# The joint pass of a four-layer graph network: sources turned on VectorE, joins and range sums as bf16 thirds, first MLP products in one bf16 pass

## The chip, the cores and the metric

The kernel runs on one core of one Trainium2 chip. The time is the device time of one execution in microseconds (us), the median of the runs of that kernel. A profile is one further execution with the hardware profiler on; its length is given beside the others, since here it differs from them. Engines: TensorE (matmul, with its weight loads apart), VectorE, ScalarE, GpSimd (which here only issues indirect DMAs), and SP, the queue that issues the plain DMAs.

## The reference

12,500 nodes with 32 features, 400,000 edges sorted by their target `dst`. Four layers, each on a normalised copy `h` of `x`, each added to `x`:

```python
h = jnp.maximum(_layernorm(x, axis=-1), 0.0)
x = x + _L0_gnn_ref(h, edge_attr_32, L0_gnn_eps, src, dst)
h = jnp.maximum(_layernorm(x, axis=-1), 0.0)
x = x + _L1_gnn_ref(h, src, dst, edge_attr_3, edge_attr_10, edge_weight, L1_gnn_W1, L1_gnn_W2)
h = jnp.maximum(_layernorm(x, axis=-1), 0.0)
x = x + _L2_gnn_ref(h, src, dst)
h = jnp.maximum(_layernorm(x, axis=-1), 0.0)
x = x + _L3_gnn_ref(h, src, dst, edge_attr_4, edge_attr_8, L3_gnn_fc_w1, L3_gnn_fc_w2)
```

Layer 1 (an equivariant convolution) is the heavy one. For every edge a small MLP makes 896 weights, which are contracted with the features of both ends and the edge's direction:

```python
h = 2.0 ** 0.5 * jax.nn.relu(emb @ W1 / 10.0 ** 0.5)
w = (h @ W2 / 16.0 ** 0.5).reshape(E, 7, MUL, MOUT)
...
edge_ftr = jnp.concatenate([s_act, (gates[:, :, None] * v_out).reshape(E, 24)], axis=1) * norm[:, None]
return jax.ops.segment_sum(edge_ftr, edge_dst, num_segments=N)
```

Layer 2 is a normalised sum in the other direction: each edge adds the scaled features of its target to its source, `segment_sum(xs[edge_col], edge_row)` with `edge_row = src` and `edge_col = dst`.

## The kernel before

Edges are padded to 196 chunks of 2048. A chunk is 16 groups of 128 edges, or four sets (`Q4`) of `B` = 512. Since edges are sorted by target, the targets of a chunk lie within 128 successive node rows, its *window*: sums by target are matmuls with a one-hot matrix `oh` into that window, and target features come from the window by a matmul with the one-hot matrix `has`. Sources are anywhere: they are gathered by indirect DMA, 128 rows each (`hs`), and layer 2's sums by source are scattered by indirect DMA with accumulation into four tables. [...] the group is first *joined*: a 128 x 128 matrix `eq` says which edges share a source, a matmul with it gives each the sum, and all but the first are sent to a spare row.

The program has three stretches: layer 0 (with `rest`, a generator of preparations that is advanced beside its loop), the joint pass of layers 1 and 2 (`edges12`), and layer 3. The change lies in the joint pass and in `rest`.

`edges12` is unrolled over the chunks and software-pipelined by hand. A round is twelve steps `s`. In round c, chunk c (`now`) gets its twelve `product(c, j, h)`: two matmuls of 64 input rows into `ps_y`, and the multiplication by `hid` into `z` on VectorE; `reduce` sums `z` over the MLP's units with four matmuls into `ps_o`. Chunk c-1 (`last`) gets `back`: `rows`, `gate`, `collect` (the sum into the window), `add`. Chunk c+1 (`next_`) gets `front`: `has`, `ends`, `times_n`, `hidden`. `gather` issues the 16 gathers of chunk c+3. Layer 2 follows behind: chunk c-3 (`close`) gets `near` (the normalisation of its window) and `lay` (target features to edges, `hd`), chunk c-4 (`far`) gets `second`: `alike` makes `eq` and the row numbers, `join` does the matmuls and evicts `summed`, `scatter` issues the 16 scatters one round later. The order on each engine is not quite that of the text: the framework that builds the program orders the instructions of each engine by a model of its own, so that GpSimd, for one, issues 16 gathers and then 16 scatters.

The parts that the change touches:

- `ends` (L718 and on): the 16 gathered groups are turned to features x edges by fp32 matmuls with the unit matrix `eye` (L723), into rows 0-31 and 64-95 of `ps_m`; target features come into rows 32-63 and 96-127 by matmuls with `has` (L727); ScalarE copies the whole to `X[:, h]` (L729). The product `Q` = `N` x `X` follows (L732).
- `hidden` (L739, L741): the MLP's first layer from `emb`, four sets of 10 rows in fp32 at partitions 0, 32, 64 and 96.
- `alike` (L871) with `firsts` (L449 to L456): `eq`, the count `cnt` of earlier equal edges through `tmp`, and the rows.
- `join` (L879, L881): fp32 matmuls of `eq` (128 x 128) with `hd` (32 columns), evicted by ScalarE.
- `collect` (L789): fp32 matmuls of `f` (32 columns as weights) with `oh` (128 columns), four column groups summed apart; `add` (L795 to L799) folds the four.

Tiles of PSUM: `ps_y` has two buffers of two banks; `ps_m`, `ps_o`, `ps_sum` and `ps_2` one bank each.

## Time and profile before

| | us |
|---|---|
| median of 3 runs | 19167.42 (19167.29 to 19172.29) |
| the profiled execution | 23109.4 |
| its span, first to last instruction | 23107.7 |

Over the span of the profiled execution TensorE is busy 15954.9 us (69%), its weight loads 8493.8, GpSimd 14407.0 (62%), VectorE 11868.8 (51%), ScalarE 5515.5 (24%); the mean granted TensorE clock is 0.828 of full speed. Busy time adds up instructions; it does not say which of them the end waited for. The chain of waits that ended last puts 39% on TensorE, 18% on VectorE, 9% on ScalarE and 5% on GpSimd. The profiled execution is a fifth longer than the runs, so a sum made in it has to be carried over with care.

An fp32 matmul appears as two records in the trace, a bf16 one as one; so 3136 x 2 records of L879 are 3136 matmuls.

### The profile page before, as it was taken

What the parts mean: (1) busy time and instruction counts of PE and PEld (TensorE: products, weight loads), DVE (VectorE), ACT (ScalarE), POOL (GpSimd) and SP (SyncE); (2) the same over time, 40 slices, a digit from 0 to 9 for tenths busy, and PEclk for the clock granted to TensorE, in tenths of its full rate; (3) what the DMA queues carried; (4) which work ended last, traced back from release to release, by engine and by line L of the source; (5) the groups of instructions that cost most, each with busy time, mean ns of one, the idle gap of its engine ahead of it and who ended that gap; (6) DMA issues with size and microseconds to landing.
All of it is one profiled execution on the core that took longest, in us unless ns stands there. A gap on an engine that the chain in (4) does not pass through costs nothing.

```text
span 23107.7 us, 229565 instructions
## 1 busy us (share of the span) xinstructions
PE 15954.9 (69%) x74484; PEld 8493.8 (37%) x74484; DVE 11868.8 (51%) x24410; ACT 5515.5 (24%) x12954; POOL 14407.0 (62%) x12552
## 2 busy tenths in 40 slices
PE   2333333328888778778777777787588888888887
PEld 2333333322333333333333333333355445445544
DVE  4443333335555555555555555555455555555555
ACT  0000000002222222222222222222233333333333
POOL 5666666655777777777777777777444444444443
PEclk9999999998777777777777777777687888888887
DMA  2111111113333333333333333333100000000000
GB/s 74 42 35 23 23 23 23 23 40 73 80 80 79 77 78 83 77 78 82 80 78 81 80 77 79 78 83 77 24 12 12 12 12 12 12 12 12 12 12 18
DMA packets 1503407, 1138.52 MB, mean 49 GB/s; under 512 B 1141492, under 2 KB 1304900, under 8 KB 1448308
## 3 DMA queue, kind: packets, MB, share of 16 engines
q1 hardware_dynamic: 745098, 891.46, 12.3%
q0 software_dynamic: 752640, 206.32, 9.7%
q10 hardware_dynamic: 4448, 25.89, 0.3%
q8 instruction: 592, 9.70, 0.2%
q14 instruction: 629, 5.15, 0.1%
HBM read 1022.56 MB, written 99.86 MB: 49 GB/s over the span
## 4 chain that ended last, share of the span: by engine, by line
PE 39%; DVE 18%; another core or an unknown queue 15%; issue 11%; ACT 9%; POOL 5%; DMA 2%; DVEq 0%; SPq 0%; POOLq 0%; ACTq 0%
PE ps_y L746 11%; PE ps_w L1162 10%; PE ps_o L756 4%; PE ps L879 4%; ACT oh L781 3%; DVE z L749 3%; DVE rb L1180 3%; POOL hs L433 2%; DVE pb L1172 2%; PE ps_h L1140 2%; ACT oh L710 2%; PE ps_win L385 2%; PE ps_sum L1201 1%; DVE f L1178 1%
## 5 line engine op out<-in xcount | busy, mean ns | idle before, releaser
L885 POOL DMA_INDIRECT acc<-summed,rows x3136 | 4995.6, 1593 | 1898.0 <-issue 1141.3
L1130 POOL DMA_INDIRECT hs<-feat,src x3136 | 3085.0, 984 | 3653.4 <-DVE pb L1172 2657.8
L1162 PE MATMUL ps_w<-w2b,hid 128*128 128x256 f32 x12544 | 4006.1, 462 | 608.6 <-issue 430.0
L433 POOL DMA_INDIRECT hs<-feat,src x3136 | 3136.5, 1000 | 1881.0 <-issue 864.2
L704 POOL DMA_INDIRECT hs<-feat,src_c x3136 | 3189.0, 1017 | 1126.7 <-issue 932.0
L1162 PEld LDWEIGHTS ps_w<-w2b,hid 128*128 128x128 f32 x12544 | 2722.3, 227 | 2283.9 <-issue 1572.6
L749 DVE TENSOR_TENSOR z<-ps_y,hid 128x1024 f32<-128x1024 f32 x2352 | 2842.0, 1218 | 1235.5 <-PE ps_y L746 1007.3
L385 PE MATMUL ps_win<-m,oh 128*128 128x32 f32 x6272 | 1488.0, 402 | 2521.3 <-ACT m L561 1829.8
L746 PE MATMUL ps_y<-X,w2t 64*128 64x512 f32 x4704 | 2258.9, 838 | 613.4 <-ACT hid L741 306.4
L385 PEld LDWEIGHTS ps_win<-m,oh 128*128 128x128 f32 x6272 | 1398.1, 328 | 2612.4 <-ACT m L561 1921.6
L1167 DVE TENSOR_TENSOR pa<-ps_w,q 128x512 f32<-128x512 f32 x784 | 536.0, 684 | 3153.4 <-PE ps_w L1162 2928.4
L756 PE MATMUL ps_o<-z,sums 128*32 128x512 f32 x9408 | 1936.9, 697 | 2.5 <-issue 1.6
L746 PE MATMUL ps_y<-Q,w2t 64*128 64x512 f32 x4704 | 1688.5, 740 | 83.6 <-DVE z L749 39.8
L723 PE MATMUL ps_m<-eye,hs 128*32 128x128 f32 x6272 | 805.2, 367 | 1048.3 <-ACT X L729 790.5
L879 PEld LDWEIGHTS ps<-hd,eq 128*128 128x128 f32 x6272 | 1048.0, 253 | 1241.9 <-issue 339.4
L879 PE MATMUL ps<-hd,eq 128*128 128x32 f32 x6272 | 1144.2, 335 | 513.7 <-DVE eq L871 197.1
L732 DVE TENSOR_TENSOR Q<-N,X 128x512 f32<-128x512 f32 x392 | 271.6, 693 | 2115.6 <-ACT X L729 1473.0
L1142 ACT ACTIVATE hid<-ps_h 128x1024 f32<-128x1024 f32 x784 | 799.8, 1020 | 2236.2 <-PE ps_h L1140 1651.5
L1172 DVE TENSOR_TENSOR pb<-ps_w,hs 128x256 f32<-128x256 f32 x3136 | 1281.8, 469 | 0.0
L1140 PE MATMUL ps_h<-emb,w1q 8*128 8x512 f32 x3136 | 1066.5, 761 | 230.0 <-DMA emb<-in_ea_c 165.1
L746 PEld LDWEIGHTS ps_y<-X,w2t 64*128 64x128 f32 x4704 | 603.4, 236 | 1658.0 <-issue 742.6
L723 PEld LDWEIGHTS ps_m<-eye,hs 128*32 128x32 f32 x6272 | 546.2, 147 | 1635.2 <-ACT X L729 929.7
(191 smaller groups left out, 18563.7 us busy)
## 6 DMA issues: line engine op xcount, KB each, us to landing
has<-loc_t SPq DMA_DIRECT2D x392, 1024.0 KB
srow<-in_src_t SPq DMA_DIRECT2D x392, 512.0 KB
hs<-feat,src POOLq DMA_INDIRECT x6272
N<-n_t SPq DMA_DIRECT2D x3136, 32.0 KB
edge_attr<-in_edge_attr SPq DMA_DIRECT2D x196, 256.0 KB
hs<-feat,src_c POOLq DMA_INDIRECT x3136
acc<-summed,rows POOLq DMA_INDIRECT x3136
emb<-in_ea_c SPq DMA_DIRECT2D x784, 20.0 KB
```

What stands on the lines that cost most here:

```text
L385: nc.tensor.matmul(c["sum"], lhsT=oh[:, k, :], rhs=feat[:, k, :], start=t0 + k == 0, stop=t0 + k == self.CT - 1)
L433: self.nc.gpsimd.indirect_dma_start(out=t[:, k, :], out_offset=None, in_=self.feats[l][:], in_offset=bass.IndirectOffsetOnAxis(ap=idx[:, t ...
L704: nc.gpsimd.indirect_dma_start(out=c["hs"][:, k, :], out_offset=None, in_=self.feats[1][:], in_offset=bass.IndirectOffsetOnAxis(ap=c["src_ ...
L746: nc.tensor.matmul(y[:, q, :], lhsT=self.w2t[64 * q : 64 * q + 64, j, :], rhs=c["Q" if j < 3 else "X"][64 * q : 64 * q + 64, h, :], start= ...
L749: nc.vector.tensor_mul(z, y, c["hid"][:, 2 * h : 2 * h + 2, :])
L756: nc.tensor.matmul(c["o", j // 3][32 * q : 32 * q + 32, :], lhsT=self.sums[:, j, :], rhs=c["z", j, q // 2][:, q % 2, :], start=j % 3 == 0, ...
L879: nc.tensor.matmul(t[:, k, :], lhsT=c["eq"][:, k, :], rhs=c["hd"][:, G * g + k, :], start=True, stop=True)
L885: nc.gpsimd.indirect_dma_start(out=self.tabs[2][k % NTAB][:], out_offset=bass.IndirectOffsetOnAxis(ap=c["rows"][:, G * g + k : G * g + k + ...
L1130: nc.gpsimd.indirect_dma_start(out=c["hs"][:, k, :], out_offset=None, in_=self.feats[3][:], in_offset=bass.IndirectOffsetOnAxis(ap=c["src" ...
L1140: nc.tensor.matmul(t[:, q, :], lhsT=self.w1q[r : r + 8, m * P : (m + 1) * P], rhs=c["emb"][r : r + 8], start=True, stop=True)
L1162: nc.tensor.matmul(w[:, k, :], lhsT=c["hid"][:, m, 4 * g + k].rearrange("p q s -> p (q s)"), rhs=self.w2b[:, m, :], start=m == 0, stop=m == 1)
L1172: nc.vector.tensor_mul(c["pb"][:, i, gs], w[:, :, lo : lo + 64].rearrange("p g (w u) -> p g w u", u=8), by[:, :, None, :].to_broadcast([P, ...
```

## The change

**Sources.** The turning by `eye` goes. VectorE transposes the gathered tile in 32 x 32 blocks, the whole of it into each half of `X`; the target rows are then written over by ScalarE. Half of the 32-row blocks belong to each side, and which edges lie where now alternates: in `X[:, 1]` the source rows are those that hold targets in `X[:, 0]`. So `w2t` gets a second copy with the sides exchanged, and the sets of a half are q = h, h + 2. Gathers use the layout of `src`, which `alike` needs too, so one load serves both.

**Thirds.** An fp32 number is split into three bf16 numbers that sum to it: a copy, a subtraction, a copy, a subtraction (`thirds` for `f`, `split` for `hd`). `eq` and `oh` are exact in bf16. A join is then one bf16 matmul with 96 columns, and a reduction over the three parts on VectorE evicts it; a range sum is one bf16 matmul with 96 weight columns, and `fold` sums the three parts.

**First MLP products.** `parts_of`, a part of `rest` in layer 0, writes the thirds of `emb` to DRAM nine times (3 parts x 3), `stacked` does the like with the weights, and `hidden` multiplies 90 bf16 rows at once.

```diff
+    def parts_of(self, pool, src, dst):
+        ...
+        for k in range(0, flat.shape[1], F):
+            ks = slice(k, k + F)
+            v = pool.tile([P, 2240], F32, name="pv", bufs=2)[:, :F]
+            nc.sync.dma_start(v, flat[:, ks])
+            yield
+            p = [pool.tile([P, 2240], BF16, name=f"pp{i}")[:, :F] for i in range(3)]
+            nc.scalar.copy(p[0], v)
+            nc.vector.tensor_tensor(v, v, p[0], op=ALU.subtract)
+            yield
+            nc.scalar.copy(p[1], v)
+            nc.vector.tensor_tensor(p[2], v, p[1], op=ALU.subtract)
+            for i in range(3):
+                for j in range(3):
+                    nc.sync.dma_start(outs[3 * i + j][:, ks], p[i])
+            yield
...
-                c["emb"] = ld.tile([P, B], F32, name="emb")
-                for q in range(Q4):
-                    nc.sync.dma_start(c["emb"][32 * q : 32 * q + 10],
-                                      self.a["ea10_c"][q, :, ds(row, 1), :].rearrange("f o e -> f (o e)"))
+                c["emb"] = ld.tile([90, Q4 * B], BF16, name="emb")
+                nc.sync.dma_start(c["emb"], self.emb10[:, :, ds(row, 1), :].rearrange("k f o e -> (k f) (o e)"))
...
-            def ends(c, h):
+            def sources(c, h):
+                nc.vector.transpose(c["X"][:, h, :], c["hs"].rearrange("p t f -> p (t f)"))
+
+            def targets(c):
                 t = ps.tile([P, B], F32, name="ps_m")
-                for k in range(4):
-                    for q in range(2):
-                        nc.tensor.matmul(t[64 * q : 64 * q + 32, k * P : (k + 1) * P],
-                                         lhsT=c["hs"][:, 4 * (2 * h + q) + k, :], rhs=self.eye, start=True, stop=True)
-                for q in range(2):
-                    e0 = (2 * h + q) * B
-                    nc.tensor.matmul(t[64 * q + 32 : 64 * q + 64, :], lhsT=c["win"], rhs=c["has"][:, e0 : e0 + B],
+                for g in range(Q4):
+                    b = g ^ 1
+                    nc.tensor.matmul(t[32 * g : 32 * g + 32, :], lhsT=c["win"], rhs=c["has"][:, b * B : (b + 1) * B],
                                      start=True, stop=True)
-                nc.scalar.copy(c["X"][:, h, :], t)
+                for g in (1, 3, 0, 2):
+                    nc.scalar.copy(c["X"][32 * g : 32 * g + 32, (g ^ 1) % 2, :], t[32 * g : 32 * g + 32, :])
...
-                    r = 32 * (2 * h + q)
-                    nc.tensor.matmul(t[:, q, :], lhsT=self.w1t[r : r + 10], rhs=c["emb"][r : r + 10],
-                                     start=True, stop=True)
+                    e0 = (2 * q + h) * B
+                    nc.tensor.matmul(t[:, q, :], lhsT=self.w1t, rhs=c["emb"][:, e0 : e0 + B], start=True, stop=True)
...
-                    j = 32 * (k % 4)
-                    nc.tensor.matmul(c["sum"][j : j + 32, 0:P], lhsT=c["f"][:, k, :], rhs=c["oh"][:, k, :],
-                                     start=k < 4, stop=k >= CT - 4)
+                    nc.tensor.matmul(c["sum"][: 3 * D, 0:P], lhsT=c["f3"][:, k].rearrange("p i f -> p (i f)"), rhs=c["oh"][:, k, :],
+                                     start=k == 0, stop=k == CT - 1)
...
+            def split(c, step):
+
+                if step == 0:
+                    c["hd3"] = sp.tile([P, CT, 3, D], BF16, name="hd3")
+                if step % 2 == 0:
+                    nc.scalar.copy(c["hd3"][:, :, step // 2, :], c["hd"])
+                elif step == 1:
+                    nc.vector.tensor_tensor(c["hd"], c["hd"], c["hd3"][:, :, 0, :], op=ALU.subtract)
+                else:
+                    nc.vector.tensor_tensor(c["hd3"][:, :, 2, :], c["hd"], c["hd3"][:, :, 1, :], op=ALU.subtract)
...
             def join(c, g):
-                t = ps.tile([P, B], F32, name="ps_2")[:, : G * D].rearrange("p (k f) -> p k f", f=D)
+                t = c["joint"] = ps.tile([P, B], F32, name="ps_2")[:, : G * 3 * D].rearrange("p (k e) -> p k e", k=G)
                 for k in range(G):
-                    nc.tensor.matmul(t[:, k, :], lhsT=c["eq"][:, k, :], rhs=c["hd"][:, G * g + k, :], start=True, stop=True)
+                    nc.tensor.matmul(t[:, k, :], lhsT=c["eq", g][:, k, :],
+                                     rhs=c["hd3"][:, G * g + k].rearrange("p i f -> p (i f)"), start=True, stop=True)
+
+            def joined(c, g):
                 c["summed", g] = sp.tile([P, G, D], F32, name="summed", bufs=2 * CG)
-                nc.scalar.copy(c["summed", g], t)
+                nc.vector.tensor_reduce(c["summed", g], c["joint"].rearrange("p k (i f) -> p k f i", i=3), AX.X, ALU.add)
```

`thirds` is `split` with `f` and `f3`. In `alike`, `eq` and `tmp` become bf16 and are multiplied with a bf16 copy `before` of `earlier`. The order within a round moves a little: `front` turns the sources at steps 1 and 2, `back` splits `f` at steps 3 to 5 and collects at steps 6 and 7, `second` makes `eq`, joins and evicts in three successive steps, and `close` splits `hd` at steps 10 and 11.

## The prediction

> **What bounds the kernel.** First the busy shares over three stretches: the first layer, the joint pass, the last layer (columns: stretch, length, busy time of TensorE, its weight loads, VectorE, ScalarE and GpSimd with instruction counts, granted TensorE clock, DMA share, GB/s).
>
> ```profile
> 0.00:5217.00 5217.00, 1845.48 (x9476) 1748.66 (x9476) 2061.70 (x6755) 305.59 (x1045) 3214.02 (x3224) 1.00 0.14 34
> 5217.00:16260.00 11043.00, 8684.15 (x42664) 3402.93 (x42664) 6240.64 (x12148) 2940.13 (x6812) 8107.99 (x6192) 0.76 0.36 79
> 16260.00:23107.00 6847.00, 5425.24 (x22344) 3342.17 (x22344) 3566.42 (x5507) 2269.78 (x5098) 3084.97 (x3136) 0.80 0.07 13
> ```
>
> The change works in the middle one, 48% of the span; the last is untouched. TensorE is the busiest there (79%), but at 0.76 of its clock, and GpSimd is close. So next the instruction groups of 7000 to 15000 us, and what GpSimd waited for there:
>
> ```profile
> L885 POOL DMA_INDIRECT acc<-summed,rows x2272 | 3610.3, 1589 | 1376.1 <-issue 843.2 <-ACT summed L881 433.1 <-DMA acc<-summed,rows 55.2
> L704 POOL DMA_INDIRECT hs<-feat,src_c x2282 | 2320.7, 1017 | 695.3 <-issue 678.2 <-DMA hs<-feat,src_c 5.5 <-PE ps_o L756 4.3
> ```
>
> 16 scatters are one chunk, so 2272 of them are 142 rounds of 8000 / 142 = 56.3 us. GpSimd's own work in a round is (3610.3 + 2320.7 + 843.2 + 678.2) / 142 = 52.5 us ("issue" is the gap between two of its instructions). It really waits 3.6 us, most of it for `summed`, the output of the joins. It is thus 93% taken, and the change neither removes nor shortens one of its instructions.
>
> Third, the same stretch by engine, beside an early round in which GpSimd is not yet behind:
>
> ```profile
> 5378.60:5414.00 35.40, 34.55 (x203) 11.95 (x204) 27.20 (x53) 14.32 (x32) 28.89 (x22) 1.00 0.38 76
> 7000.00:15000.00 8000.00, 6345.16 (x31004) 2479.93 (x31000) 4514.32 (x8818) 2159.26 (x4998) 5928.93 (x4554) 0.77 0.36 79
> ```
>
> At full clock that round took 35.4 us with TensorE busy 34.55, and it held half of a chunk's joins (16 records, 2.16 us, by the same view of L879 alone). A complete round is therefore 34.55 + 2.16 = 36.7 us of TensorE at full clock. In the steady state it is 44.7 us busy at clock 0.77. VectorE is busy 31.7 us, ScalarE 15.2. So **GpSimd is the floor (52.5), TensorE at its reduced clock is what adds the last 3.8 us.**
>
> **From the profile to the median.** The profiled execution took 23109.4 us, the median of the runs is 19167.42: 3942 less. The last layer is limited by TensorE, so I take it as equal; the first two stretches hold 9408 indirect DMAs, and 3942 / 9408 = 0.42 us for each closes the gap. That is an estimate, not a reading; it must be most of the truth, since 3136 x 1.25 us (the usual period in the first layer) + 196 x 52.5 + 6847 is already 21057. By it an unprofiled round was 56.3 - 32 x 0.42 = 42.9 us over a GpSimd floor of 39.1.
>
> **The change, part by part** (one round; TensorE at full clock).
>
> *Sources turned by VectorE.* 16 fp32 products with `eye` (L723, 32 records) go; bursts of 10 and 6 records take 0.74 and 0.50 us, so -2.5 us TensorE. Two 32x32-block transposes of 128x512 come; the nearest row, L761, is 714 ns: +1.4 us VectorE. ScalarE copies the target rows in four pieces of 512 elements instead of two (L729, 580 ns): +1.2. `targets` runs four column groups together like L863 instead of two pairs: about -0.8 TensorE.
>
> *Joins in bf16 thirds.* Before, 8 records (one group of four) take 1.08 us at full clock, 4.3 a round. After, 16 bf16 products with 96 columns. The nearest bf16 row is in the first layer:
>
> ```profile
> 2097.99 0.64 PE L585 MATMUL ps_deg<-olo,ohi 128*125 128x100 bf16 x4
> ```
>
> 0.16 us each, so 2.6: -1.7 TensorE. The eviction moves from ScalarE (4 x 266 ns, -1.1) to a VectorE sum of three over 384 PSUM elements; L451 reduces 512 in 676 ns, so I take 540 ns: +2.2. Splitting `hd` costs two ScalarE copies (about 0.65, near L729) and two VectorE subtractions (694 ns, as L732): +1.3 and +1.4.
>
> *Range sums in thirds.* The same split of `f`: +1.3 ScalarE, +1.4 VectorE. The products become 16 at 0.16 = 2.6 us instead of 4 x 0.43 = 1.7: +0.9 TensorE at most, nothing at best.
>
> *First MLP products in one bf16 pass.* Two pairs at 1.13 us (L739) become four single-pass products of 512 columns. No row has one: at worst 0.16 x 5 = 0.8 each (+1.0), at best about 0.22 each, 0.9 in all. I take 1.0, since one pass replaces several: -1.3.
>
> *`eq`, `tmp`, `before` in bf16.* The row for `tmp` says 682 ns in fp32. The Trainium skill ("VectorE: DVE Perf Modes", the perf-mode tier table) gives a two-input VectorE operation 2x on bf16 in SBUF; by it 512 elements would take some 420 ns, -1.0 us a round; by the row alone nothing. No row here is all-bf16. I take -1.0. The reduction beside it (L451) stays at 676: the same table leaves reductions at 1x.
>
> *DMA.* `emb` becomes one load of 90 x 4 KB instead of four; the `src_c` load goes, and `half` reuses it. SP was waiting, not full: nothing. The order of gathers and scatters on GpSimd is as before: 16 gathers, then 16 scatters.
>
> Sum: **TensorE 36.7 - 5.4 = 31.3 us at full clock; VectorE 31.7 + 5.4 = 37.1; ScalarE 15.2 + 2.7 = 17.9; GpSimd 52.5 profiled, 39.1 by the estimate.** Nothing but GpSimd is above 39.1.
>
> *Waits that are added.* Both transposes now sit on VectorE and need all 16 gathers; behind them in its queue are the z products, so TensorE's ps_y buffers and the next round hang on them. In the trace the gathers of two successive chunks ended at 8921.2 and 8988.7; the build's order puts the transposes after the last join output, where `has` stands at 8944 and 8994.5. The slack is 23 and 6 us. If it is used up VectorE stands, but GpSimd has its 16 scatters by then and does not. Price: nothing to 1.5 us; I take 1.
>
> *First layer.* `parts_of` adds 14 steps of 2 ScalarE copies, 2 VectorE subtractions and 9 stores (72 MB together), on engines that are 6% and 40% busy, but on the SP queue, where the just-in-time `src` loads stand; GpSimd already pauses some 8 to 10 us about every 32 gathers for them. Between 0 and 14 x 20 us; I take 50.
>
> **The clock, where a rule speaks against the change.** The granted clock here is 0.77 in the steady state and 1.00 in the packed round; between 9034.5 and 9056 us it was 0.50, just after TensorE had waited for gathers. The Trainium skill ("TensorE: Matmul & The Clock Gate", Part 1) says that a window of idleness of about 3.4 us halves the clock and a busy one restores it. By that rule a TensorE with less to do is slowed more often: always at half, 31.3 becomes 62.6 us and the change loses. By the row, 0.77 gives 31.3 / 0.77 = 40.6 us, where 36.7 / 0.77 = 47.7 stands now. At half clock TensorE is soon saturated again by the products (busy 21.50 of 21.50 us in that stretch), which restores the clock, so I take the row, and keep the rule for the rival.
>
> **The forecast.** Profiled, a round falls from 56.3 to about 53.3 (52.5, and little of the waiting): 3.0 x 196 = 590, less 50 in the first layer: 23109 to about 22570. Unprofiled, VectorE's 37.1 is near the 39.1 floor, so more waiting stays: 42.9 to 40.5, 2.4 x 196 = 470, less 50: **19167 - 420 = 18750 us** (2.2% faster). Its own range is 18450 to 19050. Chance 0.50.
>
> **Rivals.**
> 1. *GpSimd was no floor without the profiler* (0.14): if its instructions cost still less, the old round was limited by TensorE. The last layer's length leaves up to 46 us for it; then 46 to about 40, 6 x 196 = 1180: 18000. For: TensorE 79% busy. Against: GpSimd's 93% taken.
> 2. *Nothing to win* (0.08): GpSimd sets both rounds, or VectorE's 5.4 us eats what TensorE gives: 19130 to 19200. For: no instruction leaves GpSimd. Against: it does wait for `summed`.
> 3. *Slower by the clock* (0.28): TensorE idles more, is released from half clock less, and joins come late to the scatters. It decides where 31.3 us over the granted clock passes 42.9, below clock 0.73. At 0.69 the round is 45.4: 2.5 x 196 + 50 = 540, 19700. For: the dips follow idleness. Against: fewer products also leave room.
>
> That the change does not do what it says has little room: the build holds the instructions counted above.
>
> **How the numbers follow.** About 0.2% (38 us) is what a measurement of this kernel can tell from no change. Faster takes the likeliest, rival 1 and a sliver of rival 2: 0.66. Within it: 0.06. Slower: rival 3, 0.28. The range goes from 18050 (just above rival 1's centre) to 19550 (near side of rival 3), leaving out some 0.07 and 0.13.
>
> **What would show it.** Right: in the joint pass GpSimd's waits for `summed` fall under 1.5 us a round, TensorE's busy time falls to some 40 us, VectorE's rises to about 37, the profiled round is near 53. Wrong: granted clock under 0.73 with GpSimd waiting more (rival 3); VectorE waiting at the transposes for `hs` with TensorE idle behind; the first layer longer by over 150 us; a profiled gain far under the unprofiled one (rival 1).

## The result, and the profile after

| | us | to the kernel before |
|---|---|---|
| before, 11 runs beside the changed kernel | 19168.49 (19160.43 to 19190.34) | |
| changed, 11 runs | 19211.08 (19192.03 to 19233.67) | 1.0024 [1.0017, 1.0032] |
| forecast | 18750 | 0.978 |

The change makes the kernel 43 us slower where 420 faster was forecast. One plain fact is needed to read everything below: **the same kernel takes 19.1 ms on some chips and 23.5 ms on others**, so every ratio here is between kernels timed on one chip. The median that the forecast started from was of the first kind, the profile that it was worked out from of the second. The execution of the changed kernel that was profiled took 19192.03 us (span 19190.3), as its other runs did: the profiler does not lengthen it.

Busy time by stretch of the changed kernel (columns as in the prediction; the middle one runs from the first to the last `z`):

```profile
0.00:4438.00 4438.00, 1873.87 (x9430) 1758.26 (x9432) 2151.70 (x6792) 369.64 (x1076) 3272.42 (x3182) 1.00 0.24 60
4438.00:14522.00 10084.00, 6832.06 (x29267) 1914.57 (x29266) 6952.09 (x13908) 3461.68 (x7175) 8207.49 (x6157) 0.78 0.44 90
14522.00:19190.00 4668.00, 4078.29 (x22464) 2793.36 (x22458) 3654.68 (x5704) 2297.12 (x5117) 3224.82 (x3215) 0.95 0.14 22
```

The same view of the kernel before, from an experiment on a chip of the first kind (run before_look, 19115.47 us):

```profile
0.00:4329.00 4329.00, 1878.58 (x9482) 1754.51 (x9484) 2091.03 (x6755) 313.34 (x1046) 3175.04 (x3175) 1.00 0.18 40
4329.00:14428.00 10099.00, 8557.06 (x42470) 3274.24 (x42468) 6185.78 (x11989) 2933.40 (x6786) 8161.30 (x6167) 0.78 0.41 85
14428.00:19113.00 4685.00, 4127.90 (x22534) 2835.28 (x22534) 3644.73 (x5667) 2294.67 (x5122) 3230.71 (x3212) 0.95 0.13 22
```

TensorE's busy time in the joint pass falls by 1725 us, as meant, and VectorE's rises by 766. The pass itself is 15 us shorter. Layer 0, which the change was only to burden a little, is 109 us longer. These two profiles come from two sets of runs, in which the kernel before differs by 61 us (19168.49 and 19106.86), so differences of this size between them need not be the change's; below, layer 0 is compared within one set. Why the joint pass does not move stands in GpSimd's groups between 6000 and 12000 us, before (run before_look) and after:

```profile
L885 POOL DMA_INDIRECT acc<-summed,rows x1834 | 2915.6, 1590 | 573.0 <-issue 499.6 <-DMA acc<-summed,rows 14.5 <-DVE z L749 14.3
L704 POOL DMA_INDIRECT hs<-feat,src_c x1838 | 1953.1, 1063 | 560.4 <-issue 519.5 <-DMA hs<-feat,src_c 23.2 <-PE ps_m L723 6.7
```

```profile
L956 POOL DMA_INDIRECT acc<-summed,rows x1835 | 3037.8, 1655 | 559.3 <-issue 515.4 <-DVE f L826 25.0 <-DMA hs<-feat,src 6.7
L757 POOL DMA_INDIRECT hs<-feat,src x1824 | 1849.1, 1014 | 556.1 <-issue 543.6 <-DMA hs<-feat,src 12.5
```

Before: 2915.6 + 1953.1 us of work and 573.0 + 560.4 of gaps, 6002 us in a stretch of 6000. Nearly every gap is the 0.3 us that lies between any two of its instructions; the waits named are under 1 us a round. GpSimd is taken all the time in the kernel *before* the change, at the same 1590 ns a scatter as in the profile that the forecast used. After it a scatter is 65 ns longer on average and a gather 49 ns shorter, which nearly cancel. The row of 16 gathers and 16 scatters makes the round, 52.3 us before and 52.4 after (stretch over the rounds in it, counted by `z`), and no instruction of it was removed.

### The profile page after: what moved, and what is told of

It is laid out like the page before. It is cut to its first block, busy times and chain, and to the rows that moved or that the text cites. A ratio compares the mean times of both kernels' runs of the same rounds, so it can differ in the third digit from the quotient of the medians.

```text
span 19190.3 us, 201806 instructions
## 1 busy us (share of the span) xinstructions
PE 12784.2 (67%) x61156; PEld 6466.2 (34%) x61156; DVE 12758.5 (66%) x26402; ACT 6128.4 (32%) x13368; POOL 14704.7 (77%) x12552
## 5 line engine op out<-in xcount | busy, mean ns | idle before, releaser
L1218 POOL DMA_INDIRECT hs<-feat,src x3136 | 3089.8, 985 | 1270.1 <-issue 887.8
L487 POOL DMA_INDIRECT hs<-feat,src x3136 | 3235.1, 1032 | 1067.3 <-issue 747.6
L757 POOL DMA_INDIRECT hs<-feat,src x3136 | 3186.1, 1016 | 1041.8 <-issue 933.8
L1250 PE MATMUL ps_w<-w2b,hid 128*128 128x256 f32 x12544 | 3056.6, 392 | 172.1 <-DVE pb L1260 172.1
L1250 PEld LDWEIGHTS ps_w<-w2b,hid 128*128 128x128 f32 x12544 | 2315.2, 192 | 1153.3 <-issue 499.7
L439 ACT CAST f<-f 128x512 bf16<-128x512 f32 x392 | 242.2, 618 | 4763.2 <-DVE f L826 4542.9
L808 PE MATMUL ps_o<-z,sums 128*32 128x512 f32 x9408 | 1731.0, 694 | 10.5 <-DVE r L813 10.1
L772 DVE STREAM_TRANSPOSE X<-hs 128x512 f32<-128x512 f32 x392 | 273.3, 700 | 2090.8 <-DMA hs<-feat,src 1937.2
L614 DVE TENSOR_TENSOR m<-hs,edge_attr 128x128 f32<-128x128 f32 x784 | 238.0, 304 | 1964.5 <-DMA hs<-feat,src 1951.3
L798 PEld LDWEIGHTS ps_y<-Q,w2t 64*128 64x128 f32 x4704 | 517.8, 254 | 2872.6 <-DVE z L801 2161.6
L615 ACT ACTIVATE m<-m 128x128 f32<-128x128 f32 x784 | 242.3, 309 | 3472.2 <-DVE m L614 2269.5
L1282 ACT ACTIVATE oh<-iota,local 128x128 f32<-128x128 f32 x3136 | 1035.4, 392 | 21.9 <-DMA edge_attr<-in_edge_attr 21.9
```

The costliest lines, as they stand in the source:

```text
L487: self.nc.gpsimd.indirect_dma_start(out=t[:, k, :], out_offset=None, in_=self.feats[l][:], in_offset=bass.IndirectOffsetOnAxis(ap=idx[:, t ...
L757: nc.gpsimd.indirect_dma_start(out=c["hs"][:, k, :], out_offset=None, in_=self.feats[1][:], in_offset=bass.IndirectOffsetOnAxis(ap=c["src" ...
L798: nc.tensor.matmul(y[:, q, :], lhsT=self.w2t[64 * q : 64 * q + 64, h, j, :], rhs=c["Q" if j < 3 else "X"][64 * q : 64 * q + 64, h, :], sta ...
L808: nc.tensor.matmul(c["o", j // 3][32 * q : 32 * q + 32, :], lhsT=self.sums[:, j, :], rhs=c["z", j, q % 2][:, q // 2, :], start=j % 3 == 0, ...
L1218: nc.gpsimd.indirect_dma_start(out=c["hs"][:, k, :], out_offset=None, in_=self.feats[3][:], in_offset=bass.IndirectOffsetOnAxis(ap=c["src" ...
L1250: nc.tensor.matmul(w[:, k, :], lhsT=c["hid"][:, m, 4 * g + k].rearrange("p q s -> p (q s)"), rhs=self.w2b[:, m, :], start=m == 0, stop=m == 1)
```

## The experiments

Seventeen runs in five sets, each set on one chip, all with the kernel before timed beside them. "Holding" is the name used below for the chips on which the kernel before takes 23.5 ms (numbers 8 and 2, the second in two sets), "undisturbed" for those with 19.1 ms (numbers 4 and 12).

| run | chip | us | before beside it | ratio, 95% |
|---|---|---|---|---|
| before_again | holding | 23644.0 (1 run) | 23624.68 | |
| before_half | holding | 24310.12 | 23624.68 | 1.0266 [1.0231, 1.0301] |
| after_half | holding | 23089.47 | 23624.68 | 0.9774 [0.9751, 0.9797] |
| after_emb_fp32 | holding | 23316.67 | 23624.68 | 0.9866 [0.9843, 0.9889] |
| before_pair | holding | 23611.86 (1 run) | 23615.13 | |
| after_pair | holding | 22753.97 | 23615.13 | 0.9638 [0.9621, 0.9655] |
| after_half_2 | holding | 23091.68 | 23615.13 | 0.9770 [0.9749, 0.9790] |
| after_emb_2 | holding | 23308.82 | 23615.13 | 0.9869 [0.9851, 0.9888] |
| before_look | undisturbed | 19115.47 (1 run) | 19106.86 | |
| before_thirds | undisturbed | 19121.76 | 19106.86 | 1.0009 [1.0000, 1.0017] |
| before_emb16 | undisturbed | 19222.65 | 19106.86 | 1.0064 [1.0048, 1.0081] |
| after_quarter | undisturbed | 17329.09 | 19106.86 | 0.9070 [0.9055, 0.9085] |
| after_last | holding | 22706.03 | 23510.12 | 0.9651 [0.9627, 0.9675] |
| after_parts3 | holding | 22537.05 | 23510.12 | 0.9585 [0.9561, 0.9608] |
| after_emb_3 | holding | 23150.55 | 23510.12 | 0.9838 [0.9813, 0.9863] |
| after_parts3_2 | undisturbed | 19091.64 | 19104.84 | 0.9993 [0.9984, 1.0001] |
| after_emb_4 | undisturbed | 19065.52 | 19104.84 | 0.9981 [0.9974, 0.9987] |

### Is the long profile the profiler's doing, and does GpSimd decide?

The first set: the kernel before, unchanged (**before_again**), and both kernels with half of the scatters left out (**before_half**, **after_half**):

```diff
             def scatter(c, g):
-                for k in range(G):
+                for k in range(G // 2):
```

> The kernel before, unchanged, profiled once more. Theory A (GpSimd already was the floor of the joint pass in the ordinary execution, and the profile shown before was of a stretched one): a span near 19170 us, rounds of about 52 us in the joint pass, GpSimd waiting for `summed` under 0.5 us a round, the last layer near 4600 us instead of 6847. Theory B (the profiler itself stretches this kernel, and only this one): a span near 23100 us again, with GpSimd waiting some 3.6 us a round and the last layer near 6850 us.

> The kernel before, with two of each four scatters left out (layer 2's sums by source are incomplete). Theory A (GpSimd is the floor, the chain of TensorE and VectorE lies not far below): 1568 scatters of about 1.9 us go, 15 us a round; the next bound, TensorE at its reduced clock, stops the fall at about 45 us a round: 17700 to 17900 us. Theory C (the chain of TensorE and VectorE limits the kernel before, GpSimd only looks full): a gain under 1%, 19000 to 19170 us.

> The changed kernel with the same two of four scatters left out. Theory A: the relief of TensorE shows once GpSimd is out of the way: a round of about 40 us, set by VectorE's 37: 16700 to 17000 us, some 900 us under the kernel before with the same scatters left out. Theory D (the change makes the chain of TensorE and VectorE no faster): within 200 us of the kernel before with half of the scatters.

All eleven timed runs of the kernel before on that chip lay between 23567 and 23690 us. So the length of the given profile is not made by profiling; it is that of some chips. And there less work for GpSimd did not help: the kernel before became 2.7% *slower* with 1568 fewer instructions on GpSimd. Whatever decides on such a chip, it is not GpSimd alone. The changed kernel with the same half left out takes 1221 us less than that, so here the work taken from the other engines does count.

### What holds the kernel up on such a chip

**before_pair** and **after_pair** are the two kernels, unchanged, beside each other.

> The kernel before, unchanged, beside the changed kernel on one chip. Theory E (TensorE is held up on some chips, for reasons that its granted clock does not show; the shown profile of before and the 23.6 ms runs are of such a chip): either 19150 to 19200 us with the signal after a group of matmuls coming about 0.4 us after the last recorded start in layer 0, or 23000 to 24000 us with signals that come 7 to 30 us late; nothing between. Theory F (what is long in the shown profile is GpSimd's or the DMA queues' slowness): if it is 23 ms again, gathers and scatters take longer than 1.25 and 1.86 us from one to the next; if it is 19.2 ms they take less.

> The changed kernel, unchanged, on the same chip as the kernel before. Theory E: on a chip that holds TensorE up, TensorE decides, and the change, which takes about 18% of its instructions, gains: ratio 0.97 to 0.99. On a chip that does not, GpSimd's row of indirect DMAs decides in both kernels: ratio 1.001 to 1.004. Theory F (GpSimd decides on every chip): ratio 1.000 to 1.004 on both.

The timeline of before_pair in layer 0 shows it (start, length, engine, line, tiles; in brackets the idle time before and what ended it). First a hold, as such a stretch is called from here on, then the same two instructions some 37 us on:

```profile
2048.67 0.64 PE L585 MATMUL ps_deg<-olo,ohi 128*125 128x100 bf16 x4
...
2068.72 0.26 DVE L588 TENSOR_TENSOR deg<-deg,ps_deg 125x100 f32<-125x100 f32 x1 [18.41 <-remote]
...
2085.30 0.64 PE L585 MATMUL ps_deg<-olo,ohi 128*125 128x100 bf16 x4
2085.98 0.26 DVE L588 TENSOR_TENSOR deg<-deg,ps_deg 125x100 f32<-125x100 f32 x1 [0.91 <-PE ps_deg L585]
```

VectorE waits for TensorE's signal that `ps_deg` is there. At 2085 it comes 0.04 us after the last of the four matmuls' recorded end, at 2049 it comes 19.4 us after. "remote" is what the view says when it finds no releaser: by the records TensorE had long been done. The trace's record of TensorE's signals says the same in bulk. Between 1000 and 4000 us of before_look every one comes within 0.42 us of the start of the last matmul before it; between 1000 and 5000 us of before_pair one in ten comes over 17 us after it, the latest 31.2. The recorded signals of VectorE and ScalarE are prompt on both chips (99 of 100 come within 0.1 us of a sender's end). What stands still, the signal or the work, can be read from a second hold of the same timeline:

```profile
2071.92 1.91 PE L385 MATMUL ps_win<-m,oh 128*128 128x32 f32 x8
2073.65 0.64 PE L585 MATMUL ps_deg<-olo,ohi 128*125 128x100 bf16 x4
...
2080.05 0.69 DVE L382 TENSOR_TENSOR oh<-iota,local 128x512 f32<-128x512 f32 x1 [7.28 <-remote]
2080.20 0.18 ACT L388 COPY wsum<-ps_win 128x32 f32<-128x32 f32 x1 [8.33 <-remote]
```

Four matmuls that signal start between 2071.21 and 2073.98; their four signals come between 2080.02 and 2080.23. Signals of work that takes 2.8 us arrive within 0.2 us, so here the work seems to have been done and its signals to have been late. Everything that needs them stands behind. TensorE's own waits in layer 0 show the same hole from the other side. Before_pair, 1000 to 5000 us (total, times, longest):

```profile
PE ps_win L385 <- ACT m L561: 1591.6, 239, 31.8
PE ps_win L385 <- issue: 597.7, 98, 26.0
```

and before_look, 1000 to 4000 us:

```profile
PE ps_win L385 <- ACT m L561: 1406.6, 507, 3.6
```

The many short waits of the second, none over 3.6 us, are the normal rhythm of a stage that GpSimd paces; the first has half as many, up to 31.8 us long. Its row "issue" (no releaser found) is not waiting for nothing: 91 of these 98 matmuls start 0.05 us after an `m` of ScalarE ends, so it is the same wait, for work that itself stood behind a late signal. The traces of holding chips lack records of signals, so that the view finds no releaser: before_pair has 14322 of VectorE's 21423, 6167 of ScalarE's 7358 and 8556 of TensorE's 10592, before_look all but 0.2%. In layer 3 the disturbance is seen in the row of its short matmuls, before_pair (17500 to 22500 us) and before_look (15200 to 18700 us):

```profile
L1201 PE MATMUL ps_sum<-oh,f 128*32 128x128 f32 x4576 | 397.1, 287 | 677.9 <-issue 615.2 <-DVE pa L1167 39.9 <-DVE f L1188 22.7
```

```profile
L1201 PE MATMUL ps_sum<-oh,f 128*32 128x128 f32 x5088 | 171.9, 276 | 67.0 <-DVE f L1188 67.0
```

Instructions of nearly the same length, but with 615 us, in gaps of at most 1.9 us, before which the trace shows nothing that TensorE could have waited for. Here the matmuls' starts themselves are drawn out. What this comes to by stretch, before_pair and then after_pair:

```profile
0.00:5361.00 5361.00, 1842.74 (x9482) 1749.26 (x9484) 2033.11 (x6755) 309.33 (x1046) 3193.15 (x3224) 1.00 0.15 33
5361.00:16376.00 11015.00, 8661.32 (x42472) 3382.15 (x42468) 6167.27 (x11989) 2926.77 (x6786) 7962.14 (x6117) 0.76 0.37 78
16376.00:23610.00 7234.00, 5429.16 (x22534) 3442.04 (x22534) 3642.30 (x5667) 2297.66 (x5122) 3222.63 (x3212) 0.77 0.08 14
```

```profile
0.00:5307.00 5307.00, 1840.66 (x9430) 1752.93 (x9432) 2111.43 (x6792) 363.55 (x1076) 3208.28 (x3182) 1.00 0.19 50
5307.00:15514.00 10207.00, 6851.87 (x29267) 1914.70 (x29266) 6960.79 (x13908) 3461.74 (x7175) 8201.51 (x6159) 0.78 0.42 89
15514.00:22723.00 7209.00, 5379.45 (x22464) 3396.88 (x22458) 3652.94 (x5704) 2300.23 (x5117) 3224.01 (x3213) 0.77 0.08 14
```

Against before_look the kernel before loses 1032 us in layer 0, 916 in the joint pass and 2549 in layer 3, 4497 in all, and GpSimd's and VectorE's busy times are the same to 3%. In layer 0 the granted clock does not tell it: it is 1.00 on both. In layer 3 it does in part: 0.77 against 0.95, and TensorE's busy time is 1301 us longer, half of what is lost there. Whether the lower clock is a cause or follows from late signals is not shown. On such a chip the change is worth 808 us in the joint pass, where a round falls from 57.1 to 52.6 us, and 3.6% in all. GpSimd's groups between 7000 and 15000 us, before_pair and after_pair:

```profile
L885 POOL DMA_INDIRECT acc<-summed,rows x2240 | 3561.7, 1590 | 1499.4 <-issue 769.0 <-ACT summed L881 621.1 <-DMA acc<-summed,rows 55.7
L704 POOL DMA_INDIRECT hs<-feat,src_c x2235 | 2259.7, 1011 | 681.1 <-issue 667.4 <-DMA hs<-feat,src_c 5.2 <-PE ps_o L756 3.4
```

```profile
L956 POOL DMA_INDIRECT acc<-summed,rows x2437 | 4012.0, 1646 | 742.6 <-issue 686.8 <-DVE z L801 20.4 <-DVE near L872 8.2
L757 POOL DMA_INDIRECT hs<-feat,src x2439 | 2502.9, 1026 | 743.6 <-issue 736.6 <-DMA hs<-feat,src 7.0
```

After the change the row fills the 8000 us here too (8001 with its gaps).

**after_half_2** (the half of the scatters again) and **after_emb_2**, beside them, are the changed kernel less a part. The second is the same kernel as after_emb_fp32 of the first set: first products in fp32 as before, and no `parts_of`.

```diff
-        self.w1t = keep.tile([90, P], BF16, name="w1tk")
+        self.w1t = keep.tile([P, P], F32, name="w1tk")
...
-            yield from self.parts_of(pool, self.a["ea10_c"], self.emb10)
...
-                    nc.tensor.matmul(t[:, q, :], lhsT=self.w1t, rhs=c["emb"][:, e0 : e0 + B], start=True, stop=True)
+                    nc.tensor.matmul(t[:, q, :], lhsT=self.w1t[r : r + 10], rhs=c["emb"][r : r + 10],
+                                     start=True, stop=True)
```

> The changed kernel with half of the scatters left out (their sums are not added). Theory E: on a chip that does not hold TensorE up, GpSimd's round falls from 52.3 to about 37.5 us (8 scatters of 1.86 us less), and TensorE or VectorE, at some 40 to 45 us, decides next: 1000 to 1700 us less than the changed kernel. On a chip that holds TensorE up: within 2% of the changed kernel. Theory F: 1.9 ms less on both.

> The changed kernel with its first products in fp32 passes as before and no preparation of thirds in layer 0. If the preparation costs what it takes in layer 0: 30 to 60 us less than the changed kernel on a chip that does not hold TensorE up, since the joint pass waits for GpSimd in either. If the 43 us come from the joint pass's longer scatters: equal to the changed kernel. On a chip that holds TensorE up, more TensorE work: 0 to 200 us more than the changed kernel.

> The changed kernel without its bf16 pass for the first MLP products: fp32 products of 10 rows again, no thirds written in layer 0. Theory A with the loss of 0.24% put down to layer 0's 72 MB of stores and their place on the SP queue: 19160 to 19180 us, back at the kernel before, with the joint pass as long as in the changed kernel. Rival (the loss is in the joint pass, for instance scatters stretched by a busier VectorE): 19200 to 19230 us, as the changed kernel.

Half of the scatters gone made the changed kernel 338 us slower than after_pair (23091.68 to 22753.97), as it had made the kernel before slower. In the joint pass of before_half the round is 61.1 us where that of before_again, on the same chip, is 57.0, and the granted clock 0.73 where it is 0.76:

```profile
7000.00:15000.00 8000.00, 5888.48 (x28549) 2216.90 (x28548) 4141.63 (x8107) 1976.12 (x4583) 3689.51 (x3144) 0.73 0.28 71
```

GpSimd is busy 46% of this stretch, and TensorE gets no more done. Why these rounds get longer with less work for GpSimd is not shown; the lower granted clock goes with it. The fp32 first products cost 555 us on a holding chip, where 0 to 200 had been expected. In the profiles of after_pair and after_emb_2 418 us of it lie in the joint pass, 2.1 us a round, where the forecast had taken 1.3 at full clock.

### Which part costs what on an undisturbed chip

The third set fell on an undisturbed chip. **before_look** is the kernel before. **before_thirds** is it with the joins and range sums by bf16 thirds alone (`thirds`, `split`, `alike`, `join`, `joined`, `collect` and `add` of the changed kernel), **before_emb16** it with the first products in one bf16 pass alone (`parts_of`, `stacked`, `hidden`). **after_quarter** is the changed kernel with three of four scatters left out, `range(G // 4)`.

> The kernel before, unchanged. Theory E (TensorE is held up on some chips; elsewhere GpSimd's row of indirect DMAs sets the joint pass): on a chip where it takes 19.2 ms, the joint pass of its profile lasts 10000 to 10100 us, GpSimd's gathers and scatters follow each other at 1.25 and 1.86 us without long gaps, and TensorE's signals come under 1.2 us after the last recorded start. On a chip where it takes 23.6 ms, the same as the two profiles of such chips already taken. Rival G (GpSimd's instructions are longer under the profiler, as the prediction took it): 1.25 and 1.86 us from one to the next cannot be fitted into a 19.2 ms run.

> The kernel before with one part of the change alone: joins and range sums by bf16 thirds. Theory E on a chip that holds TensorE up: a gain, but smaller than that of the first products in one bf16 pass (555 us between the changed kernel without and with it), in the ratio of the TensorE times reckoned in the prediction (0.8 to 1.3 us a round): about 340 us, 23270. On a chip that does not: within 0.2% of the kernel before. Rival (VectorE's extra 5 us decide): slower than before on both.

> The kernel before with another part alone: the first products of the MLP in one bf16 pass, with the preparation in layer 0. Theory E on a chip that holds TensorE up: 400 to 600 us faster than before, as in the changed kernel. On a chip that does not: 0 to 50 us slower than before, by the preparation in layer 0, and then this part explains the 43 us of the result.

> The changed kernel with three of four scatters left out (their sums are not added): GpSimd's round falls from 52.3 to about 27.5 us. Theory E on a chip that does not hold TensorE up: the joint pass falls until VectorE (37 us of work a round) or TensorE sets it, 40 to 44 us a round, total 17000 to 17600. On a chip that holds TensorE up: no faster than the changed kernel with half of the scatters (23090), since TensorE decides and is held up more when it gets its work sooner. If GpSimd decides on such a chip as well: 2 ms under the changed kernel.

The thirds make no difference, 1.0009, though they take 669 us off TensorE's busy time (14563.5 to 13894.5 in the first 19110 us of the two profiles). The first products cost 116 us where 0 to 50 had been expected: 69 in layer 0 and 69 in the joint pass by the profiles (layer 3 gives 26 back). In the joint pass GpSimd's scatters are longer (1609 ns on average, 1594 before, some 46 us in all) and its pauses over 0.4 us come to 102 us instead of 70; what lengthens them is not shown. After_quarter is the test of the bound itself. Without three quarters of the scatters:

```profile
6000.00:12000.00 6000.00, 4684.71 (x20992) 1312.88 (x20996) 5006.09 (x10079) 2505.96 (x5179) 3345.21 (x2800) 0.83 0.39 106
```

The round falls to 42.9 us, VectorE is busy 83% of it (35.8 us), TensorE 78% (33.5 us), GpSimd 56%: the other engines' work lies well under GpSimd's 52.4, and shows only when GpSimd's is taken away.

### Where the loss lies, and a version without it

**after_parts3** stores each third of the embedding once instead of three times, 24 MB in layer 0 instead of 72, and loads it three times in each round:

```diff
-            for i in range(3):
-                for j in range(3):
-                    nc.sync.dma_start(outs[3 * i + j][:, ks], p[i])
+            for i in range(3):
+                nc.sync.dma_start(outs[i][:, ks], p[i])
...
-                nc.sync.dma_start(c["emb"], self.emb10[:, :, ds(row, 1), :].rearrange("k f o e -> (k f) (o e)"))
+                for j in range(3):
+                    nc.sync.dma_start(c["emb"][30 * j : 30 * j + 30],
+                                      self.emb10[:, :, ds(row, 1), :].rearrange("k f o e -> (k f) (o e)"))
```

**after_emb_3** and **after_emb_4** are the kernel of after_emb_2 again, **after_last** is the changed kernel, **after_parts3_2** the kernel of after_parts3. The first three ran on a holding chip, the other two on an undisturbed one.

> The changed kernel, unchanged, as the mark for the two beside it. Undisturbed chip: ratio to the kernel before 1.002 to 1.006, layer 0 about 70 to 110 us longer, the joint pass within 20 us. Chip that holds TensorE up: 0.96 to 0.97.

> The changed kernel with each third of the embedding stored once and loaded three times, instead of stored three times and loaded once: 24 MB of stores in layer 0 instead of 72, two loads more a round. If the stores' traffic is what slows layer 0's gathers: about two thirds of the 70 to 110 us come back, 45 to 75 us less than the changed kernel on an undisturbed chip. If it is the number of steps on SP's queue or the arithmetic: 0 to 20 us less. On a chip that holds TensorE up: within 0.3% of the changed kernel.

> The changed kernel with fp32 first products and no preparation. If the preparation is the whole loss: 70 to 120 us less than the changed kernel on an undisturbed chip, that is within 0.2% of the kernel before, and no better than it, since GpSimd sets layer 0 and the joint pass in both. If the joint pass loses as well: less of it comes back. On a chip that holds TensorE up: 2 to 2.5% more than the changed kernel, as measured on another such chip.

> The same kernel as after_parts3. On an undisturbed chip, if the stores' traffic slows layer 0's gathers: layer 0 some 30 to 50 us longer than before's 4329 us instead of 109, total ratio 0.999 to 1.001. If it is SP's queue or the arithmetic: ratio as the changed kernel's, 1.002 or more. On a chip that holds TensorE up: 0.955 to 0.965, as before.

> The changed kernel with fp32 first products and no preparation. On an undisturbed chip, if the preparation is the whole loss: ratio 0.997 to 1.001 and layer 0 as before's 4329 us. If the joint pass loses as well: above 1.001. On a chip that holds TensorE up: 0.98 to 0.99.

Layer 0 up to the first `z` is 4329 us in before_look and, on the same chip, 4398 in before_emb16 and 4406 in after_quarter, which have the whole preparation. It is 4438 in the changed kernel of the result, whose chip is not on record, and on another undisturbed chip 4385 in after_parts3_2 and 4328 in after_emb_4. So without the preparation the loss in layer 0 is gone, and a third of the stores gives back 13 to 20 us of some 70: layer 0 is still 56 us longer than before_look's, where 30 to 50 had been expected. One profile tells little below that: before_thirds, with layer 0 unchanged, has 4346. Where the loss arises is seen in a window of layer 0, of before_look, before_emb16, the changed kernel, after_parts3_2 and after_emb_4 in turn:

```profile
1250.00:2000.00 750.00, 342.43 (x1728) 320.06 (x1728) 361.98 (x1211) 51.85 (x182) 574.48 (x576) 1.00 0.15 29
```

```profile
1250.00:2000.00 750.00, 315.00 (x1590) 300.09 (x1589) 405.97 (x1152) 101.34 (x195) 588.67 (x530) 1.00 0.42 139
```

```profile
1250.00:2000.00 750.00, 315.95 (x1593) 301.08 (x1593) 405.12 (x1152) 101.38 (x196) 588.93 (x529) 1.00 0.43 140
```

```profile
1250.00:2000.00 750.00, 316.13 (x1597) 301.13 (x1596) 399.70 (x1153) 100.88 (x195) 587.50 (x534) 1.00 0.27 77
```

```profile
1250.00:2000.00 750.00, 345.30 (x1744) 322.77 (x1744) 364.84 (x1223) 52.24 (x183) 573.24 (x581) 1.00 0.15 29
```

The last bracket is GpSimd's gathers: 576 without the preparation, 530 and 529 with it, at 1.3 us each some 60 us. They are not fewer because GpSimd waits; its busy time is higher, so each gather takes longer (589 / 529 = 1.11 us, not 1.00). With a third of the stores, 77 GB/s instead of 140, they are 534: in this window little comes back, so the volume of the stores is not what slows the gathers most here; the number of DMAs under way or VectorE's and ScalarE's extra work may be, and that was not taken apart. The changed kernel's further 32 to 40 us over before_emb16 and after_quarter are not the stores': between 2500 and 3750 us, when the preparation has been over since 1878 us, it starts 190 to 192 gathers in each 250 us, before_emb16 and after_parts3_2 194 to 196. That belongs to its chip or its execution.

So there are two better versions. That of after_parts3 is 4.1% faster than before on a holding chip, more than the changed kernel's 3.5% there (0.7% between the two, where 0.3% at most had been expected), and not distinguishable from before on an undisturbed one. That of after_emb_4 is 0.2% faster there, and 1.3 to 1.6% on holding chips. The 39 us that after_emb_4 gains with layer 0 unchanged must come from behind layer 0; no profile of the kernel before exists from that chip to say where. What it has over before_thirds (1.0009) is the turning of the sources by VectorE, which was not run alone. The parts do not add up to the whole: 116 us lost in before_emb16 and 39 won in after_emb_4 make 77, where the result is 43. The 69 us that before_emb16 loses in the joint pass are the part that is not understood.

## Why the prediction was wrong

**The step that failed** is "From the profile to the median". It put 3942 us down to "0.42 us for each" of 9408 indirect DMAs and said: "The last layer is limited by TensorE, so I take it as equal". Limited by TensorE it is (91% busy in the row below), and TensorE is what differs between the two kinds of chip. The last layer of before_look, cut at the same instructions as in the forecast:

```profile
14630.00:19113.00 4483.00, 4091.42 (x22344) 2807.03 (x22344) 3574.78 (x5508) 2285.11 (x5098) 3098.18 (x3136) 0.96 0.12 20
```

The forecast's profile has 6847 us there: 2364 of the 3994 us between the two profiles lie in a stretch without a scatter (890 and 740 in the first two). An indirect DMA costs about the same in both (scatters 1589 and 1590 ns, gathers 1017 and 1063). So the unprofiled floor of 39.1 us did not exist, the round of the timed runs was not 42.9 us but 52.3, GpSimd's own 52.5, and there was hardly anything above the floor to win. The sum printed beside that step said so in part: 3136 x 1.25 + 196 x 52.5 + 6847 came to more than the median. The first two terms are measured periods of an engine that runs at its own pace; the one that could give was the third.

**"GpSimd is the floor (52.5)"** was right, to 0.3 us, on both kinds of chip. That it is so close is in part luck: the 843.2 us of "issue" in it are 161 us more than 2272 gaps of 0.3 us, 1.1 us a round, and the longer gathers of before_look (1063 ns for 1017) make up for 0.7 of that. The second half of the sentence, "TensorE at its reduced clock is what adds the last 3.8 us", was wrong: before_look has the same clock, 0.78, TensorE 85% busy, and no such waits. The late signals of a holding chip come with them. Rival 2, "GpSimd sets both rounds", is what happened in the joint pass, at a chance of 0.08; the time lies 11 us above its range because of layer 0.

**What the change does to the engines** was right in kind. On a chip like that of the profile, GpSimd's waits for `summed` (621.1 us in before_pair, 4.4 a round) were to fall under 1.5 us a round: they are gone, and no named wait in its list is over 0.2. The round was to be near 53 us: 52.6. VectorE was put at 37 us: 35.9 (5467.78 / 8000 x 52.55). `tmp` in bf16 takes 415 ns against 682, where 420 had been estimated from the table in the Trainium skill ("VectorE: DVE Perf Modes", the perf-mode tier table), and the reduction `cnt` stays at 674, as that table has it: here it and this trace agree. The sum of three takes 546 ns against 540. TensorE was mis-sized: about 40 us busy forecast, 35.2 measured (5353.27 / 8000 x 52.55). The terms too small were the turning by `eye` (4.2 us busy a round in before_pair, where 2.5 at full clock is 3.2 at 0.77), the joins (5.8 to 1.7 us busy a round in before_pair and after_pair, 4.1 less, where 1.7 at full clock is 2.2 at 0.77) and the targets (3.0 to 1.1, where 0.8 was taken); the range sums, booked as +0.9, became 0.4 shorter. On that chip the forecast of 23109 to 22570, a ratio of 0.977, stands beside 0.9638 [0.9621, 0.9655]: the waits went as forecast and the gain was greater, since the round before was 57.1 there, not 56.3, and TensorE's relief was greater. But what made the joins late there had been put down to the clock.

**Layer 0** was priced at 50 us between 0 and 280; on one chip it cost 69 (before_emb16) and 76 (after_quarter), and no more than 109. The mechanism named, SP's queue with its just-in-time loads, was not it: in after_quarter GpSimd has no gap over 0.4 us between 217 and 4358 us of layer 0, preparation and all, so most of the 76 us are longer gathers. The whole layer 0 of before_look has 4 such gaps, that of the forecast's profile 99. So the pauses of "8 to 10 us about every 32 gathers" that the forecast took for waits on loads came with the holding chip.

**Rival 3, slower by the clock**, did not occur. TensorE's busy share of the joint pass fell from 85% to 68% on undisturbed chips, and the granted clock is 0.78 in both; on before_look's chip it even rose, to 0.83, in after_quarter (78% busy between 6000 and 12000 us). The prediction's reading of the rule in the Trainium skill ("TensorE: Matmul & The Clock Gate", Part 1), that a TensorE with less to do is slowed more often, would have lowered it; in this range it did not. And where GpSimd sets the pace, a lower clock costs nothing until TensorE fills the round too. By an estimate from its 34.9 us of busy time a round (6832.06 us in 196 rounds) at 0.78, that would need a clock near 0.52.

**Rival 1** falls with the same step: GpSimd's instructions are no shorter without the profiler.

## What to carry to other kernels

A profile and a median that differ by a fifth need not be two views of the same state of the chip; before the gap is shared out over instructions, ask which stretch of the profile could be shorter at all, and leave alone the engine that already runs back to back at a constant period. When one engine's busy time and its constant gaps add up to the stretch, as GpSimd's did here, work taken from any other engine is worth nothing until that row gets shorter. A preparation placed "beside" a stage that is paced by DMA issues is not free, even if its engines are idle: here it lengthened the gathers themselves. And before "issue" or "remote" is read as an engine that waits for nothing, look what ended just before the instruction: in layer 0 it was mostly an ordinary wait for ScalarE.

## What the runs showed of the hardware

- On two of the chips used (in three sets of runs) TensorE's signals come up to 31 us after its last recorded matmul start, and the whole kernel is 23% longer; on the other chips they do not. The granted clock reads 1.00 through it in layer 0. In layer 3, where matmul starts are drawn out as well, it is 0.77 against 0.95. The traces of such chips also lack 24 to 39% of VectorE's signal records, those of the others under 0.5%. The Trainium skill ("TensorE: Matmul & The Clock Gate", "Seeing it yourself") warns that clock events in a trace can be unreliable and tells of a rate stuck at a quarter for over 50 us; whether this is that, no run here tells. Instruction fetching was no different: the same number and size of packets for the same kernel on either kind of chip. The cause stays open.
- On such a chip less work on GpSimd made both kernels slower (2.7% the kernel before, 1.5% the changed one).
- GpSimd's indirect DMAs of 128 rows of 128 bytes follow each other at 1.25 us for a gather and 1.85 us for an accumulating scatter at best, 0.30 us of it a gap, on both kinds of chip. Gathers are longer beside the preparation in layer 0, 1.11 us on average instead of 1.00, with 139 GB/s of DMA traffic and with 77 (1.10) alike; what of the preparation does it was not taken apart.
